# A four-layer graph network on one core: the prologue in a new order, and six more steps of the second pair's front inside it

## The chip, the cores and the metric

The kernel runs on one core of a Trainium2 chip (trn2). The core has TensorE (PE) for matrix products, VectorE (DVE), ScalarE (ACT) and GpSimd (POOL) for elementwise work and reductions, and SyncE (SP), which issues transfers; ScalarE issues transfers too. Each engine runs its own instructions in the order in which the program gives them. The metric is the device time of one execution in microseconds; lower is better.

## The reference

Thirty-two graphs `x` of 512 nodes with 64 features share one weighted adjacency matrix `adj` (512 x 512). Four layers follow each other, each as `x = x + layer(relu(layernorm(x)))`:

```python
# layer 0, three steps; node 0 is first set to an intervention value
effects = einsum('nm,bmd->bnd', adj, v)
v = relu(concat([v, effects]) @ W1.T + b1) @ W2.T + b2
# layer 1, twice
z = relu((adj @ z) @ weights[i])
# layer 2, eight heads, then the same once more with W_out
h = x @ W;  s = (h @ h.T) * graph;  s = where(s == 0, -1e16, s)
out = softmax(s) @ h + b          # leaky_relu(0.01) after it
# layer 3; adj has its diagonal set to 1
h = x @ weight;  e = leaky_relu(e_src + e_dst, 0.2) * adj
out = softmax(e) @ h + bias
```

Layers 2 and 3 hold most of the work: for every graph nine 512 x 512 score matrices with a softmax over the graph in layer 2, and one in layer 3.

## The kernel before

Two graphs are worked on together as a pair; there are 16 pairs. Nodes lie on the partitions in four blocks of 128, and the two graphs' features lie side by side, 128 wide. Everything is in float32, except for the mask (`NEGM`) and the small identity (`I2b`), which are bfloat16.

The program has three parts. A **prologue** issues the loads and prepares shared operands. The **ticks**, ten for each pair, hold the attention work: in every tick each unit of heads has its scores (L427, and L430 for the mask), maxima (L448), exponentials (L459), normalisations (L471), turns (L477) and weighted sums (L487). The order inside a tick is written out by hand in a table, `PLACES`: a step's name gives the tick that it belongs to and its place there. A **tail** finishes the last pair.

Layers 0 and 1 of a pair are a generator, `front(p, state)`, whose 24 yields cut it into steps counted from 0. Steps 0 and 1 are the first normalisation, 2 its end, 3 a transpose. Each of the three steps of layer 0 is three front steps: `by_nodes` (L329) into PSUM; `v` copied by ScalarE (L353) or added to `ubc` by VectorE (L355); then L363 and `aggregated` (L317) into one bank and ReLU to `hT` (L366). These are front steps 4 to 12. Step 13 adds the residual (`x1`, L370) and issues the load of the pair after next. Steps 14 to 16 normalise (VectorE: L264, L266, L273, L275, L281; POOL: L268, L270, L277), 17 to 20 are layer 1 (L317, `eT` at L380, L329 with `NP`; `x2` at L388), 21 to 23 normalise again. At the end `features_of` transposes z (L401, ZZ at L403) and `values_of` issues the 16 transfers of `quarters` (L299). The keys of the attention (L804, Y at L814) come before the scores.

In the ticks the front of the next pair is spread over the table as names `F0` to `F24`. The first pair's front runs in the prologue, and the second pair's first six steps are called there too, one after each of the first pair's steps 6 to 11 (`HEAD = 6`); its further steps, from `F6`, lie in the ticks of the first pair.

Between the first pair's steps the prologue calls the functions that prepare operands, by the dictionary `among`: `weights_turned` (L175 to L180: W1 and W2 transposed, copied to W1T and W2T by ScalarE), `biases` (L191 to L193), `weights_joined` (L198 to L204: products of W2 with W1 and with the biases), `graph_turned` (L186, L187: 16 transposes of `A` and four copies to `AT` by ScalarE), `masks` (L209 to L212), `factors` (L230: one quarter each of the graph copy `A2`), `grams` (L237 to L243), `vectors` (L247 to L255).

Transfers are issued from two queues. SP loads x of the first pair, `A` (L124), x of the second, then NP (L143), Wh (L145), A2 (L147), the small weights of layer 3 (L149 to L151), W_out (L152) and A3 (L154). ScalarE loads W1 (L132), W2 (L133), the bias rows (L136, L137), the intervention value (L139) and b2 spread over the partitions (`b2bc`, L140). In the program each transfer takes one of eight completion counters in turn, and waits until the transfer before it on the same counter has landed.

Of the kernel before, what the change touches and what calls it, by code (L numbers as in the profile page):

```python
# [9 lines left out]
BF16 = mybir.dt.bfloat16  # L10
AF = mybir.ActivationFunctionType
ALU = mybir.AluOpType
AX = mybir.AxisListType

P = 128
# [6 lines left out]
def gnn_stack_kernel(  # L22
# [36 lines left out]
    nc = tc.nc  # L59
    B, N, D = x.shape  # L60
# [8 lines left out]
    R = tuple(slice(j * D, (j + 1) * D) for j in range(2))  # L69

    def blk(t):
        return slice(t * P, (t + 1) * P)

    def hblk(s):
        return slice(s * D, (s + 1) * D)

    const = ctx.enter_context(tc.tile_pool(name="const", bufs=1))
# [8 lines left out]
    def mm_ps():  # L86

        return ps_m.tile([P, N], F32, tag="mm", name="mm")
# [16 lines left out]
    ident = const.tile([P, P], F32, name="ident")  # L105
    mhalf = const.tile([P, NT * 2], F32, name="mhalf")
    ivt = const.tile([1, 2, D], F32, name="ivt")

    early1 = hp.tile([P, 4, P], F32, tag="h3T", bufs=1, name="early1")
    W1n, W2n, ones = early1[:, 0:2], early1[:, 2], early1[:, 3]  # L110
# [9 lines left out]
    rows, b2rep = early2[0:NB, 0], early2[:, 1]  # L120
# [6 lines left out]
    make_identity(nc, ident)  # L127
    for z0, value in ((mhalf, -0.5), (ones, 1.0), (NP, 0.0), (w3a, 0.0), (a1bd, 0.0), (a2bd, 0.0)):
        nc.gpsimd.memset(z0, value)
    for j, r in enumerate(R):  # L130
        for k in range(2):
            nc.scalar.dma_start(out=W1n[r, k, r], in_=W1[:, k * D : (k + 1) * D])  # L132
        nc.scalar.dma_start(out=W2n[r, r], in_=W2)  # L133
    for k, b in enumerate((b1, b2, b_out, bias3)):
        for r in R:
            nc.scalar.dma_start(out=rows[H + k : H + k + 1, r], in_=b.rearrange("(o d) -> o d", o=1))  # L136
    nc.scalar.dma_start(out=rows[0:H, :], in_=bh)  # L137
    for j in range(2):
        nc.scalar.dma_start(out=ivt[:, j, :], in_=iv)  # L139
        nc.scalar.dma_start(out=b2bc[:, 0, j, :], in_=b2.partition_broadcast(P))  # L140
    xts[1] = load_x(1)
    for r in R:
# [15 lines left out]
    W1T = const.tile([P, 2, 2, P], F32, name="W1T")  # L158
    W2T = const.tile([P, P], F32, name="W2T")
    cols = const.tile([P, NB], F32, name="cols")  # L160
    b1c, b2c, boc, b3c = (cols[:, H + k : H + k + 1] for k in range(4))
    ubc = const.tile([P, 1, P], F32, name="ubc")
    b1s = const.tile([P, 1], F32, name="b1s")
    b1k = (b1c, b1s)
    AT = const.tile([P, NT, N], F32, name="AT")
    II = const.tile([P, 2, D], F32, name="II")
    II2 = II.rearrange("p k d -> p (k d)")
    I2b = const.tile([P, D], BF16, name="I2b")
    NEGM = const.tile([P, NT, N], BF16, name="NEGM")
    a2rep = const.tile([P, P], F32, name="a2rep")  # L170
    G = const.tile([P, H, D], F32, name="G")
# [10 lines left out]
    def graph_turned():  # L182
        for s in range(NT):
            pt = mm_ps()
            for t in range(NT):
                nc.tensor.transpose(pt[:, blk(t)], A[:, t, blk(s)], ident)  # L186
            nc.scalar.copy(AT[:, s, :], pt)  # L187

    def biases():
        pt = mm_ps()  # L190
# [4 lines left out]
    def weights_joined():  # L195
        pt = mm_ps()
        for k in range(2):
            nc.tensor.matmul(pt[:, blk(k)], lhsT=W2n, rhs=W1T[:, k, 0, :], start=True, stop=True)  # L198
        nc.tensor.matmul(pt[:, 2 * P : 3 * P], lhsT=b2rep, rhs=W1T[:, 1, 0, :], start=True, stop=True)
        nc.tensor.matmul(pt[:, 3 * P : 3 * P + 1], lhsT=W1T[:, 0, 0, :], rhs=b2c, start=True, stop=True)  # L200
        for k in range(2):
            nc.vector.tensor_copy(W1T[:, k, 1, :], pt[:, blk(k)])
        nc.vector.tensor_copy(ubc[:, 0, :], pt[:, 2 * P : 3 * P])
        nc.vector.tensor_tensor(b1s, pt[:, 3 * P : 3 * P + 1], b1c, ALU.add)  # L204

    def masks():

        for k in range(2):
            nc.vector.tensor_tensor(II[:, k, :], ident[:, 0:D], ident[:, D:P], ALU.add)  # L209
        nc.vector.tensor_copy(I2b, II[:, 0, :])  # L210

        nc.vector.tensor_scalar(NEGM, A, 0.0, NEG_INF, ALU.is_equal, ALU.mult)  # L212

# [14 lines left out]
    def factors(k):  # L228
        a2 = A2[:, 2 * k : 2 * k + 2, :]
        nc.vector.scalar_tensor_tensor(a2, a2, 0.0, a2, ALU.is_equal, ALU.add)  # L230

    def grams():

        WT = hp.tile([P, H, D], F32, tag="us", bufs=1, name="WT")
        pt = mm_ps()
        for h in range(H):
            nc.tensor.transpose(pt[:, hblk(h)], Wh2[0:D, h, :], ident[0:D, 0:D])  # L237
        nc.vector.tensor_copy(WT.rearrange("p h d -> p (h d)"), pt)
        pt = mm_ps()
        for h in range(H):  # L240
            for r in R:
                nc.tensor.matmul(pt[r, hblk(h)], lhsT=WT[:, h, :], rhs=WT[:, h, :], start=True, stop=True)
        nc.vector.tensor_copy(G.rearrange("p h d -> p (h d)"), pt)  # L243

    def vectors():
        for j in range(2):
# [549 lines left out]
    def keys(ua, ub):  # L796
# [22 lines left out]

    state = {p: {} for p in range(NPAIR)}  # L820
    first, second = front(0, state), front(1, state)
    HEAD = 6
    among = {
        0: [weights_turned],
        1: [biases, weights_joined, graph_turned],
        7: [masks],
        8: [lambda: factors(0)],
        9: [lambda: factors(1)],
        10: [lambda: factors(2)],
        11: [lambda: factors(3)],  # L830
        14: [grams],
        15: [vectors],
    }
    for n, _ in enumerate(first):
        for fn in among.get(n, ()):
            fn()
        if 6 <= n < 6 + HEAD:
            next(second)


# [80 lines left out]
    def at(t, name, fn):  # L921
        dt, place = PLACES.get(name, (1, 0))
        if t + dt < LEAD and name[0] in "FZ":

            dt, place = LEAD - t, PLACES["s1a"][1] + 0.01 * (len(jobs[LEAD]) + 1)
        token = f"{owner[0]}:{name}"
        if token in TAIL and (t + dt >= END or owner[0] in list("epqrsEU")):
            dt, place = END + 1 - t, TAIL.index(token)
        jobs.setdefault(t + dt, []).append((place, fn))
# [34 lines left out]
    for p in range(NPAIR):  # L964
# [31 lines left out]
        if p + 1 < NPAIR:  # L996
            steps = second if p == 0 else front(p + 1, state)
            for n in range(HEAD if p == 0 else 0, 25):
                at(base, f"F{n}", lambda steps=steps: next(steps, None))
# [50 lines left out]
```

## Time and profile before

| what | value |
|---|---|
| median of 3 runs | 2333.57 us (2332.89 to 2333.98) |
| profiled execution | 2338.17 us, span 2336.3 us |
| mean granted TensorE clock | 0.976 |
| TensorE busy | 2186.7 us, 94% of the span |
| VectorE busy | 1857.4 us, 80% |
| ScalarE busy | 1493.1 us, 64% |
| POOL busy | 1299.6 us, 56% |
| first scores (L427) of the first pair start | 82.88 us |
| first weighted sum (L487) starts | 107.82 us |
| TensorE busy from 200 to 300 us | 99.10 of 100 us |

The page describes one execution in microseconds. A line such as `L317` is a line of the kernel; `mm<-AT,v` names the tile written and those read. In the slices the span is cut into 40 equal parts, each digit the busy share in tenths. The list of windows gives busy microseconds (and instructions) of TensorE, its weight loads, VectorE, ScalarE and POOL in a stretch, then the granted clock, the share of time in which the transfer engines were busy, and GB/s. The chain of waits goes back from the last instruction to what released it, step by step.

### The profile page before, as it was taken

The page shows a single profiled execution, that of the slowest core. Times are in us where ns is not written, and L with a number is a line of the kernel's source. Part 1 is how long each engine was busy: PE and PEld are TensorE (multiplying, and loading weights), DVE is VectorE, ACT ScalarE, POOL GpSimd, SP SyncE. Part 2 cuts the span into 40 slices and gives each one's busy share as a digit, 9 for nine tenths or more (in the row PEclk, how much of TensorE's full clock was granted, in tenths as well). Part 3 has the DMA queues.
Part 4 walks back from the last instruction along what each step waited for, and adds up shares of the span by engine and source line. Part 5 has one row for each costly group of instructions (what it writes and reads, how often), then busy time and mean ns, then how long its engine had stood idle before and what let it go on. Part 6 is the DMA issues. An engine that isn't in the chain of part 4 may idle for free.

```text
span 2336.3 us, 78517 instructions
## 1 busy us (share of the span) xinstructions
PE 2186.7 (94%) x32683; PEld 1172.3 (50%) x32683; DVE 1857.4 (80%) x4100; ACT 1493.1 (64%) x3752; POOL 1299.6 (56%) x2175
## 2 busy tenths in 40 slices
PE   6889999999999999999999999999999999999863
PEld 3435555555555555555555555555555555555342
DVE  3558788879888888988888898888888898887653
ACT  1346557667676766767676676767666676766544
POOL 2345465656666565565656466565656556655342
PEclk9899999999999999999999999999999999999886
DMA  5001111202121120212112021211202111211112
GB/s 122 11 15 21 25 20 23 42 14 39 21 41 26 24 42 13 41 21 39 25 27 40 13 42 21 37 25 29 39 15 42 20 31 25 31 32 19 22 25 46
DMA packets 279047, 70.20 MB, mean 30 GB/s; under 512 B 275100, under 2 KB 276132, under 8 KB 278692
## 3 DMA queue, kind: packets, MB, share of 16 engines
q1 hardware_dynamic: 277888, 65.02, 16.8%
q8 instruction: 256, 4.19, 0.8%
q14 instruction: 99, 0.81, 0.1%
q10 hardware_dynamic: 804, 0.17, 0.0%
HBM read 10.49 MB, written 4.19 MB: 6 GB/s over the span
## 4 chain that ended last, share of the span: by engine, by line
PE 76%; ACT 9%; DVE 6%; POOL 2%; SPq 2%; issue 1%; DMA 1%; ACTq 0%; DVEq 0%; POOLq 0%
PE s L427 20%; PE mm L487 17%; PE mm L317 9%; ACT sm L459 6%; PE mm L550 5%; PE mm L756 5%; PE mm L521 5%; PE s L430 5%; DVE sm L477 4%; PE mm L329 3%; PE mm L804 3%; SPq L299 2%; PE mm L363 1%; DVE sm L448 1%; PE mm L593 1%
## 5 line engine op out<-in xcount | busy, mean ns | idle before, releaser
L459 ACT ACTIVATE sm<-sm,nmx 128x512 f32<-128x512 f32 x1280 | 911.0, 720 | 238.5 <-POOL nmx L455 238.2
L471 POOL TENSOR_SCALAR sm<-sm,rs 128x512 f32<-128x512 f32 x1280 | 869.8, 699 | 149.1 <-DVE rs L469 109.0
L448 DVE CUSTOM_DVE_ANT_0 sm<-s,A 128x512 f32<-128x512 f32 x1152 | 734.0, 679 | 146.3 <-PE s L430 119.8
L477 DVE STREAM_TRANSPOSE sm<-sm 128x1024 f32<-128x1024 f32 x640 | 769.4, 1224 | 39.5 <-POOL sm L471 38.4
L427 PE MATMUL s<-ZZ,Y 64*64 64x512 f32 x4096 | 572.1, 605 | 24.9 <-ACT Y L814 14.0
L487 PE MATMUL mm<-sm,vq 32*64 32x256 f32 (+1 forms) x17152 | 502.7, 380 | 26.0 <-DVE sm L477 18.3
L455 POOL TENSOR_SCALAR nmx<-mx 128x2 f32<-128x2 f32 x640 | 148.3, 235 | 600.6 <-DVE mx L448 544.7
L487 PEld LDWEIGHTS mm<-sm,vq 32*64 32x64 f32 x17152 | 401.8, 135 | 141.7 <-issue 55.9
L427 PEld LDWEIGHTS s<-ZZ,Y 64*64 64x64 f32 x4096 | 146.9, 132 | 250.2 <-issue 112.9
L430 PE MATMUL s<-NEGM,I2b 64*64 64x512 bf16 x2304 | 257.9, 378 | 0.0
L459 ACT ACTIVATION_READ_ACCUMULATOR sm<-sm,nmx 128x1 f32 x1280 | 251.2, 196 | 0.0
L542 ACT COPY us<-mm 128x256 f32<-128x256 f32 x256 | 76.2, 382 | 156.6 <-PE mm L487 156.4
L317 PE MATMUL mm<-AT,v 128*128 128x512 f32 x384 | 173.6, 595 | 0.0
L532 ACT ACTIVATE y<-mm,cols 128x512 f32<-128x512 f32 x256 | 159.2, 684 | 11.1 <-PE mm L521 11.0
L268 POOL TENSOR_TENSOR xc<-x,nmu 128x512 f32<-128x512 f32 x48 | 54.8, 1141 | 192.1 <-DVE nmu L266 192.1
L430 PEld LDWEIGHTS <-I2b 64*64 64x64 bf16 x2304 | 81.0, 107 | 159.8 <-issue 159.2
L521 PE MATMUL mm<-us,Wh 64*64 64x512 f32 x1024 | 133.9, 592 | 23.1 <-ACT us L542 23.1
L277 POOL TENSOR_TENSOR r<-ve,mhalf 128x8 f32<-128x8 f32 x64 | 110.8, 1731 | 44.9 <-DVE ve L275 41.1
L756 PE MATMUL mm<-sm,vq 32*64 32x256 f32 x3712 | 118.0, 380 | 10.2 <-DVE sm L477 8.8
L550 PE MATMUL mm<-y,Wo_sb 128*64 128x512 f32 x512 | 126.9, 605 | 0.0
L317 PE MATMUL mm<-AT,z 128*128 128x512 f32 x256 | 120.1, 613 | 2.1 <-DVE z L281 1.4
L317 PEld LDWEIGHTS mm<-AT,v 128*128 128x128 f32 x384 | 73.2, 191 | 93.3 <-issue 91.7
(134 smaller groups left out, 2002.0 us busy)
## 6 DMA issues: line engine op xcount, KB each, us to landing
vq<-z SPq DMA_DIRECT2D x512, 32.0 KB, 1.9
vq<-hn SPq DMA_DIRECT2D x512, 32.0 KB, 1.9
vq<-h3n SPq DMA_DIRECT2D x512, 32.0 KB, 1.9
A<-in_adj_dram SPq DMA_DIRECT2D x5, 1024.0 KB
xt<-in_x_dram SPq DMA_DIRECT2D x32, 128.0 KB, 2.3
out_dram<-xo SPq DMA_DIRECT2D x32, 128.0 KB, 2.9
src<-src SPq DMA_DIRECT2D x64, 1.0 KB, 1.9
Wh<-in_L_gnn_Wh_dram SPq DMA_DIRECT2D x2, 256.0 KB
```

What stands on the lines that cost most here:

```text
L317: nc.tensor.matmul(pe, lhsT=v[:, m].rearrange("p j d -> p (j d)"), rhs=AT[:, m, :], start=(first and m == 0), stop=(m == NT - 1),)
L427: nc.tensor.matmul(pss[half][R[ab], :], lhsT=lhsT, rhs=rhs, start=True, stop=False)
L430: nc.tensor.matmul(pss[half][R[ab], :], lhsT=I2b[R[half], :], rhs=NEGM[R[half], k, :], start=False, stop=True,)
L448: nc.vector.tensor_tensor_reduce(self.sm[:, s, :], src, graph, 1.0, -FMAX, ALU.mult, ALU.max, self.mx[:, s : s + 1])
L459: nc.scalar.activation(self.sm[:, s, :], self.sm[:, s, :], AF.Exp, bias=self.nmx[:, s : s + 1], accum_out=self.ssum[:, s : s + 1],)
L471: nc.gpsimd.tensor_scalar(self.sm[:, s, :], self.sm[:, s, :], self.rs[:, s : s + 1], 1.0, ALU.mult, ALU.mult)
L477: nc.vector.transpose(out=two, in_=two)
L487: nc.tensor.matmul(self.u[i][R[c], 0 : weights.shape[1] * 32], lhsT=values[32 * i : 32 * i + 32, jb, :], rhs=weights[32 * i : 32 * i + 32, ...
L521: nc.tensor.matmul(py[c][r, :], lhsT=Wh2[R[c], 2 * (self.q - 1 + c) + ab, r], rhs=self.us[R[c], 2 * ab : 2 * ab + 2].rearrange("p i (s e) ...
L532: nc.scalar.activation(y, py[c], AF.Prelu, bias=cols[:, h : h + 1], alpha=0.01)
L550: nc.tensor.matmul(pa[R[ab], :], lhsT=Wo_sb[:, h, :], rhs=self.y[h], start=(k == 0), stop=(k == 1),)
L756: nc.tensor.matmul(self.u[i][r, 0 : N // 2], lhsT=values[i // 2][q, jb, :], rhs=sm[q, :, 32 * jb : 32 * jb + 32], start=(jb == 0), stop=(j ...
```

## The change

Arithmetic and results stay; the order of the prologue changes, and who does some of its copies.

- W1 is loaded with one transfer for each half of the partitions instead of two. The intervention value is loaded earlier.
- `I2b` is copied by ScalarE straight from the identity, between its transfers, and no longer cast on VectorE in `masks`.
- `graph_turned` runs before `biases` and `weights_joined`; two of its four copies go to VectorE. `weights_joined` is cut in two: the part with the biases becomes `biases_joined` and runs four steps later.
- `grams` copies on ScalarE instead of VectorE.
- `masks` moves from step 7 to 9, the four `factors` from 8 to 11 to 16 to 19, `vectors` from 15 to 17.
- Twelve steps of the second pair's front run in the prologue instead of six: the new ones (`F6` to `F11`, two `by_nodes`, two `v`, two aggregations with `hT`) stand after the first pair's steps 14, 15, 16, 21, 22 and 23. They leave the ticks of the first pair.

```diff
-    for j, r in enumerate(R):
-        for k in range(2):
-            nc.scalar.dma_start(out=W1n[r, k, r], in_=W1[:, k * D : (k + 1) * D])
+    for r in R:
+        nc.scalar.dma_start(out=W1n[r, :, r], in_=W1.rearrange("o (k d) -> o k d", k=2))
         nc.scalar.dma_start(out=W2n[r, r], in_=W2)
+    for j in range(2):
+        nc.scalar.dma_start(out=ivt[:, j, :], in_=iv)
+
+    I2b = const.tile([P, D], BF16, name="I2b")
+    for r in R:
+        nc.scalar.copy(I2b[r], ident[r, r])
     for k, b in enumerate((b1, b2, b_out, bias3)):
         for r in R:
             nc.scalar.dma_start(out=rows[H + k : H + k + 1, r], in_=b.rearrange("(o d) -> o d", o=1))
     nc.scalar.dma_start(out=rows[0:H, :], in_=bh)
     for j in range(2):
-        nc.scalar.dma_start(out=ivt[:, j, :], in_=iv)
         nc.scalar.dma_start(out=b2bc[:, 0, j, :], in_=b2.partition_broadcast(P))
...
-            nc.scalar.copy(AT[:, s, :], pt)
+            (nc.scalar.copy, nc.vector.tensor_copy)[s % 2](AT[:, s, :], pt)
...
-        nc.tensor.matmul(pt[:, 2 * P : 3 * P], lhsT=b2rep, rhs=W1T[:, 1, 0, :], start=True, stop=True)
-        nc.tensor.matmul(pt[:, 3 * P : 3 * P + 1], lhsT=W1T[:, 0, 0, :], rhs=b2c, start=True, stop=True)
-        for k in range(2):
             nc.vector.tensor_copy(W1T[:, k, 1, :], pt[:, blk(k)])
-        nc.vector.tensor_copy(ubc[:, 0, :], pt[:, 2 * P : 3 * P])
-        nc.vector.tensor_tensor(b1s, pt[:, 3 * P : 3 * P + 1], b1c, ALU.add)
+
+    def biases_joined():
+        pt = mm_ps()
+        nc.tensor.matmul(pt[:, 0:P], lhsT=b2rep, rhs=W1T[:, 1, 0, :], start=True, stop=True)
+        nc.tensor.matmul(pt[:, P : P + 1], lhsT=W1T[:, 0, 0, :], rhs=b2c, start=True, stop=True)
+        nc.vector.tensor_copy(ubc[:, 0, :], pt[:, 0:P])
+        nc.vector.tensor_tensor(b1s, pt[:, P : P + 1], b1c, ALU.add)
...
-        nc.vector.tensor_copy(I2b, II[:, 0, :])
...
-        nc.vector.tensor_copy(WT.rearrange("p h d -> p (h d)"), pt)
+        nc.scalar.copy(WT.rearrange("p h d -> p (h d)"), pt)
...
-        nc.vector.tensor_copy(G.rearrange("p h d -> p (h d)"), pt)
+        nc.scalar.copy(G.rearrange("p h d -> p (h d)"), pt)
...
-    HEAD = 6
+
+    BESIDE = (6, 7, 8, 9, 10, 11, 14, 15, 16, 21, 22, 23)
+    HEAD = len(BESIDE)
     among = {
         0: [weights_turned],
-        1: [biases, weights_joined, graph_turned],
-        7: [masks],
-        8: [lambda: factors(0)],
-        9: [lambda: factors(1)],
-        10: [lambda: factors(2)],
-        11: [lambda: factors(3)],
+        1: [graph_turned],
+        2: [weights_joined],
+        3: [biases],
+        5: [biases_joined],
+        9: [masks],
         14: [grams],
-        15: [vectors],
+        16: [lambda: factors(0)],
+        17: [lambda: factors(1), vectors],
+        18: [lambda: factors(2)],
+        19: [lambda: factors(3)],
     }
     for n, _ in enumerate(first):
         for fn in among.get(n, ()):
             fn()
-        if 6 <= n < 6 + HEAD:
+        if n in BESIDE:
             next(second)
```

More of the change, by code (lines that the diff above doesn't have):

```diff
@@ L167, in gnn_stack_kernel @@
     II2 = II.rearrange("p k d -> p (k d)")
-    I2b = const.tile([P, D], BF16, name="I2b")
     NEGM = const.tile([P, NT, N], BF16, name="NEGM")
```

## The prediction

> **What bounds the kernel now.** I read the page's busy table and slices first. TensorE is 94% busy, and its row of the slices shows where it isn't: the first slices and the last.
>
> ```profile
> PE 2186.7 (94%) x32683; PEld 1172.3 (50%) x32683; DVE 1857.4 (80%) x4100; ACT 1493.1 (64%) x3752; POOL 1299.6 (56%) x2175
> PE   6889999999999999999999999999999999999863
> PEclk9899999999999999999999999999999999999886
> ```
>
> So TensorE work is dear after the ramp and nearly free in the prologue (0 to 82.9 us). The chain that ended last, in order of time, shows what the prologue waits for. Columns: start, length, what.
>
> ```profile
> 3.62 5.95 DMA early<-in_L_gnn_W_dram
> ...
> 26.27 5.25 DMA Wo_sb<-in_L_gnn_W_out_dram
> 31.52 1.22 DVE A L230
> ...
> 42.59 0.70 DVE x L370
> ...
> 50.14 6.71 PE mm L317 x8
> ...
> 64.98 0.70 DVE x L388
> ...
> 76.78 2.00 PE mm L363 x2
> 78.78 4.17 PE mm L317 x8
> ...
> 100.21 3.45 PE mm L317 x8
> ```
>
> The reader sees a serial chain: weights until 9.6; a graph copy (A2) that lands at 31.5 and holds VectorE; two normalisations (from 42.59 and 64.98) in which TensorE waits; then a piece of the second pair's front (76.78 to 82.95) ahead of the first scores. L317 takes 6.71 us at 50.14 and 3.45 later, for the same eight records. The windows say why: busy time by engine, then the granted clock.
>
> ```profile
> 42.60:50.10 7.50, 2.68 (x43) 2.13 (x43) 4.96 (x12) 0.00 (x0) 3.73 (x3) 0.73 0.17 37
> 50.10:65.00 14.90, 12.71 (x32) 5.89 (x32) 0.02 (x1) 1.77 (x3) 0.00 (x0) 0.79 0.00 0
> 65.00:73.00 8.00, 0.00 (x0) 0.00 (x0) 3.08 (x6) 0.00 (x0) 4.33 (x4) 0.59 0.00 1
> 73.00:82.90 9.90, 9.22 (x34) 3.99 (x34) 0.00 (x0) 1.66 (x3) 0.00 (x0) 0.64 0.30 49
> 96.00:108.00 12.00, 11.10 (x70) 4.77 (x74) 11.44 (x23) 7.38 (x21) 6.75 (x14) 1.00 0.01 1
> ```
>
> TensorE idles 5 us and 8 us, and comes back at a clock of 0.6 to 0.8. From 96 to 108 VectorE, too, is full (11.44 of 12).
>
> The list of waits on ScalarE for the first 45 us has one more:
>
> ```profile
> ACT L179 <- DMA ivt<-_intervention_value_dram: 12.5, 1, 12.5
> ```
>
> ScalarE issues 19 transfers itself. Its first compute stands behind all of them, with the 1.28 us table load (12.53 to 13.81); only then is W1T copied.
>
> **What the Trainium skill says.** "TensorE: Matmul & The Clock Gate", Part 1, says that an idle TensorE falls to half its clock after about 3.4 us and needs about as long of activity to come back: the trace agrees (8.06 us idle, then L363 at 2.07 for 1.02). The same part calls ScalarE's and VectorE's queues strict FIFO, so a waiting instruction holds all behind it; the trace agrees (L281 and L309 behind L230 at 31.5). "DMA: Bandwidth & Descriptors", Anatomy of one DMA, says that a transfer's semaphore wait happens on the issuing sequencer: the trace agrees (SP's xt waits 5.9 us for a weight). Its fixed cost of about 2.0 us fits xt (2.3 to landing), not the weights (5.9) or NP (4.2).
>
> **The change part by part.**
>
> *Transfers.* In both programs each transfer takes one of eight completion counters in turn and waits for the one before on that counter. Two transfers fewer (2 x 0.62 us of issue) shift every later assignment. W1's bytes stay, so weights land about 9.5 as now. Then ScalarE, in order: ivt; table load and two I2b copies (not in the trace; 0.19 to 0.43 each by the ScalarE copies there, I take 0.25; hidden, since all end near 6 and the weights land at 9.5; uncovered they cost 0.5, not less than nothing); b1 waits for the last W2 (9.5); the second b2 waits for xt1 (issued near 8.4, +2.3: 10.7); b_out waits for both NP transfers (issued 8.8 to 10.3, +4.2: 13 to 14.5); bias3 and bh by 15; b2bc waits for the second Wh half. Wh is queued behind NP on SP; its first half took from 12.46 to 20.4 now, with A2 and b2bc in flight. In the new order A2 itself waits for Wh, so I take 16.5 and bound it 14.5 to 20. The W1T copies then start near 17.0 (bounds 15 to 20.5), against 13.82. That is an added wait; behind it on ScalarE stand W1T, W2T, AT and zT, and TensorE and all the first pair wait for zT.
>
> *Graph turned first.* The 16 transposes (3.3 us) run from 9.5, when A has landed, instead of 15.87. VectorE takes two of the four AT copies (2 x 0.58). zT then starts 0.43 + 0.28 + 1.16 = 1.9 after W1T: 18.9, against 19.69, a gain of 0.8. biases_joined now lies between by_nodes and L363: 0.63 + 0.43 us of records, 0.85 on TensorE's path. Sum: 0; the first hT stays at 25.9.
>
> *factors moved.* At 31.52 L230 held z of the second pair, so L309 and L329 began 1.1 later than hT allowed (33.07 to 34.21). The four factors (4 x 1.2) now follow the first z of the norm, where A2 is long there: gain 1.1. If b2bc lands late (18.07 now, perhaps 22), POOL's L337, xc and sq and then VectorE's v and ve run 4 us later and end near 27.5, still just ahead of L355 at 27.85. x1 comes at 41.5 (42.59). The cast of I2b (about 0.15) leaves VectorE at a place with slack: nothing.
>
> *First normalisation*, counted from x1. z is ready at +7.45, now as before. TensorE: Wh transposes to +0.6, WT copy on ScalarE to +1.25, Gram matmuls to +2.45, then the second pair's L363 and L317 (0.9 + 3.45) to +6.75, hT on ScalarE to +7.5, by_nodes to +8.7. So L317 of the first pair starts at +8.7 instead of +7.55, but warm: 3.7 instead of 6.7. Then w3's transpose and L254, which waits for w3T behind VectorE's a2rep, hold L329 0.8 longer than eT would. x2 comes at +21.0, now +22.39. Gain 1.4.
>
> *Second normalisation.* x2 to the end of z's copy stays at 7.98. L363, L317, hT and by_nodes (6.3) fit in; VectorE's v stands behind z and costs nothing there, since scores need Y later. L401 (1.11 to 0.6) and L804 (1.98 to 1.1) run warm: 1.4 less. L363 and L317 are gone from between keys and scores: 6.2 less (76.71 to 82.88). Instead the scores wait for Y, which those hid: 1.0 more. Gain 6.6.
>
> So the first scores come 1.1 + 1.4 + 6.6 = 9.1 earlier, at 73.8.
>
> *Ramp.* Steps F6 to F11 leave the ticks: L363 and L317 at 99.1 (4.6), two by_nodes (2 x 1.1), two v (2 x 0.65), hT. That is 6.8 us of TensorE, but VectorE sets the pace from 84 to 108, so the gain is its own: 0.9 where by_nodes delayed the third pair of scores (88.00), 0.6 for v at 106.62. I take 1.3 (0.3 to 5: nothing but v if the rest refills, nearly all of TensorE's share if VectorE catches up). From the first weigh (107.82) both orders are the same, TensorE is 99% busy, and the lead is kept.
>
> Sum: 9.1 + 1.3 = 10.4. The profiled execution has 2338.17 us around its span of 2336.3, 0.2% over the median of 2333.57; so it would become 2327.8, and the median **2323.2**.
>
> **Rivals.**
>
> *1, likeliest (0.72).* As worked out: a gain of 7 to 13, by W1T at 15 to 19.5 and the ramp's bounds.
>
> *2, late transfers (0.14).* Wh or NP land as late as now, W1T starts at 20 to 23, b2bc comes so late that POOL holds VectorE's v. For it: a Wh half took 7.9 us. Against: A2's 2 MB are no longer beside it. 3 to 6 us lost of 10.4: about 2328.5.
>
> *3, more comes through (0.08).* Transfers land in 2.3 us each, so W1T starts at 14 (3 us more), and TensorE's freed time counts in the ramp (2 more): 2317 to 2319.
>
> *4, slower (0.04).* ScalarE stands at b2bc until Wh's second half lands, and that comes only after the A2 halves, which landed at 26.3 and 31.4. Every us of W1T after 17.0 passes to the end; the gain is gone from 27.4, and with W1T at 32.5 the time is 10.4 - 15.5 = 5 us worse: 2338.7. Against: Wh is issued ahead of A2, and the first A2 half waits for the first Wh half.
>
> *5, it does not do what it says (0.02).* TensorE's fillers don't keep the clock up, or the lead is absorbed at a later wait on VectorE (126 to 131): within 0.2%. For: VectorE is 80% busy. Against: its order there is unchanged, so it leads too.
>
> **Numbers.** A measurement can tell about 0.2% (4.7 us) from no change, so faster means under 2328.9. Case 1, case 3 and most of case 2 are faster: 0.90. The rest of 2, and 5: 0.06. Case 4: 0.04. The range runs from case 3's 2317.5 to case 2's 2328.5.
>
> **What would show it.** In the new profile: AT's transposes from about 9.5; W1T copies at 15 to 19.5 with a wait on transfers just before; no VectorE wait on A2; L317 of the first z at 3.7 us and a clock near 1.0 from 42 to 80; x2 near 62.5; first scores near 74; the first weigh near 97.4. W1T after 22, or cold L317s after the norms, would make the forecast wrong; so would a first weigh later than 104.

## The result and the profile after

| | before | after |
|---|---|---|
| median of 20 runs | 2333.66 us (2329.20 to 2336.53) | 2329.24 us (2325.23 to 2334.82) |
| profiled execution, span | 2338.17, 2336.3 us | 2334.82, 2333.0 us |

The ratio is 0.9984, 95% interval 0.9978 to 0.9991: 4.4 us by the medians, where 10.4 were forecast, and the median lies above the range of 2317.5 to 2328.5. The profiled execution of after is the longest of its twenty, so its times are read against other executions further down. Lines of after stand four further on than those of before from L230 on: L317 is now L321, L329 L333, L363 L367, L366 L370, L370 L374, L388 L392, L427 L431, L448 L452, L487 L491, L521 L525.

The page of after: busy table, TensorE's slices, granted clock.

```profile
PE 2189.5 (94%) x32683; PEld 1170.6 (50%) x32683; DVE 1857.3 (80%) x4099; ACT 1493.9 (64%) x3754; POOL 1298.6 (56%) x2175
PE   7889999999999999999999999999999999999873
PEclk9899999999999999999999999999999999999886
```

The averages barely move: TensorE is 2.8 us busier with the same work, and the clock's second slice is still an 8. The chain of waits of after, its first 140 us (start, length, what):

```profile
9.96 3.74 DMA Wh<-in_L_gnn_Wh_dram
...
14.13 10.14 DMA b2bc<-in_L_gnn_b_dram
24.41 1.26 POOL xt L341
...
27.82 0.70 DVE v L277
...
28.71 0.60 DVE v L359
29.36 3.71 PE mm L321 x8
...
43.54 1.88 PE mm L246 x32
45.42 1.92 PE mm L367 x2
...
64.47 0.70 DVE x L392
...
75.95 1.99 PE s L431 x8
78.37 1.71 PE s L431 x8
...
102.61 10.04 PE mm L491 x248
...
129.05 8.92 PE mm L491 x250
```

The graph copy A2 and the lone L363 and L317 ahead of the scores are gone; the scores start 6.9 us earlier than in the first profile of before (82.88). In their place the chain shows b2bc, which lands at 24.3 and holds POOL, then VectorE's v. The products at half clock ("cold" from here on, "warm" at full clock) are still there, at other places: L246 and L367 at 43.5 to 47.3, the first scores at 1.99 for eight (1.02 warm), and the first two weighted sums at 10.04 and 8.92 (7.80 for 256 and 7.15 for 250 in before).

Windows of after (busy us of TensorE, its loads, VectorE, ScalarE, POOL; granted clock; transfers):

```profile
42.60:50.10 7.50, 6.83 (x46) 3.99 (x45) 3.30 (x7) 1.17 (x2) 3.73 (x3) 0.77 0.15 35
50.10:65.00 14.90, 12.15 (x47) 6.48 (x46) 6.00 (x10) 2.46 (x4) 0.00 (x0) 1.00 0.01 2
65.00:73.00 8.00, 5.39 (x21) 2.72 (x19) 3.17 (x7) 0.69 (x1) 4.34 (x4) 1.00 0.00 0
73.00:82.90 9.90, 8.56 (x62) 3.06 (x64) 2.80 (x9) 3.06 (x7) 0.44 (x2) 0.66 0.31 50
96.00:108.00 12.00, 9.56 (x136) 4.63 (x140) 10.42 (x22) 2.93 (x8) 7.67 (x15) 0.74 0.00 1
```

The steps beside the normalisations do fill TensorE (6.83 of 7.5 us where it had 2.68; 5.39 of 8 where it had nothing). But the clock is 0.77 beside the first normalisation, 0.66 from 73 to 83, and 0.74 from 96 to 108, a stretch that ran at 1.00 before. In the second normalisation the added steps end at 70.7 us (L333 at 69.51 for 1.16), before the wait does. Finer windows of the same ramp in after:

```profile
92.50:96.00 3.50, 1.86 (x16) 0.50 (x12) 2.97 (x7) 3.49 (x10) 1.23 (x3) 1.00 0.00 0
96.00:99.00 3.00, 2.29 (x16) 0.50 (x12) 2.97 (x7) 0.00 (x0) 3.00 (x6) 1.00 0.00 0
99.00:102.50 3.50, 1.88 (x16) 0.51 (x16) 3.50 (x6) 1.95 (x5) 1.70 (x5) 0.89 0.00 0
102.50:106.00 3.50, 3.39 (x64) 2.28 (x72) 1.96 (x8) 0.98 (x4) 1.60 (x4) 0.50 0.02 5
```

With steps F6 to F11 gone from the ticks TensorE is only half to three quarters busy while it waits for VectorE. No wait there is longer than 1.6 us, yet the clock falls, at 101.73 us, and the weighted sum that follows runs at half speed. Windows laid on the two falls, the stretch ahead of each and then the cold one:

```profile
71.01:74.42 3.41, 1.25 (x16) 0.89 (x20) 1.29 (x2) 0.58 (x1) 0.64 (x2) 1.00 0.12 19
74.42:81.25 6.83, 6.16 (x40) 1.95 (x32) 2.04 (x7) 1.07 (x2) 0.23 (x1) 0.50 0.33 53
98.32:101.73 3.41, 2.09 (x18) 0.51 (x16) 3.41 (x6) 1.18 (x3) 2.38 (x6) 1.00 0.00 0
101.73:108.56 6.83, 5.95 (x112) 3.95 (x120) 5.28 (x12) 2.13 (x7) 3.12 (x6) 0.50 0.01 2
```

### The profile page after: what moved, and what is told of

It reads as the page before. It is cut to its first block, busy times and chain, and to the rows that moved or that the text cites. A ratio compares the mean times of both kernels' runs of the same rounds, so it can differ in the third digit from the quotient of the medians.

```text
span 2333.0 us, 78520 instructions
## 1 busy us (share of the span) xinstructions
PE 2189.5 (94%) x32683; PEld 1170.6 (50%) x32683; DVE 1857.3 (80%) x4099; ACT 1493.9 (64%) x3754; POOL 1298.6 (56%) x2175
## 4 chain that ended last, share of the span: by engine, by line
PE 76%; ACT 9%; DVE 7%; POOL 3%; SPq 2%; issue 2%; DMA 1%; ACTq 0%; DVEq 0%; POOLq 0%
PE s L431 20%; PE mm L491 16%; PE mm L321 9%; ACT sm L463 6%; PE mm L554 5%; PE mm L525 5%; PE mm L760 5%; PE s L434 5%; DVE sm L481 4%; PE mm L333 3%; PE mm L808 3%; SPq L303 2%; DVE sm L452 2%; PE mm L367 1%; PE mm L597 1%
## 5 line engine op out<-in xcount | busy, mean ns | idle before, releaser
L452 DVE CUSTOM_DVE_ANT_0 sm<-s,A 128x512 f32<-128x512 f32 x1152 | 734.5, 680 | 145.0 <-PE s L434 118.9
L431 PE MATMUL s<-ZZ,Y 64*64 64x512 f32 x4096 | 574.9, 606 | 28.7 <-ACT Y L818 14.7
L491 PE MATMUL mm<-sm,vq 32*64 32x256 f32 (+1 forms) x17152 | 504.3, 381 | 28.9 <-DVE sm L481 20.2
L491 PEld LDWEIGHTS mm<-sm,vq 32*64 32x64 f32 x17152 | 400.1, 135 | 147.4 <-issue 59.1
L431 PEld LDWEIGHTS s<-ZZ,Y 64*64 64x64 f32 x4096 | 147.5, 132 | 257.2 <-issue 110.9
L321 PE MATMUL mm<-AT,v 128*128 128x512 f32 x384 | 173.1, 593 | 0.1
L536 ACT ACTIVATE y<-mm,cols 128x512 f32<-128x512 f32 x256 | 159.3, 684 | 11.0 <-PE mm L525 10.9
L525 PE MATMUL mm<-us,Wh 64*64 64x512 f32 x1024 | 134.0, 592 | 23.2 <-ACT us L546 23.2
L760 PE MATMUL mm<-sm,vq 32*64 32x256 f32 x3712 | 118.1, 380 | 10.2 <-DVE sm L481 8.8
L321 PEld LDWEIGHTS mm<-AT,v 128*128 128x128 f32 x384 | 73.3, 191 | 93.5 <-issue 92.6
L285 DVE SCALAR_TENSOR_TENSOR z<-xc,r 128x512 f32<-128x512 f32 x64 | 45.3, 708 | 92.6 <-POOL r L281 89.4
```

What stands on the lines that cost most here:

```text
L321: nc.tensor.matmul(pe, lhsT=v[:, m].rearrange("p j d -> p (j d)"), rhs=AT[:, m, :], start=(first and m == 0), stop=(m == NT - 1),)
L431: nc.tensor.matmul(pss[half][R[ab], :], lhsT=lhsT, rhs=rhs, start=True, stop=False)
L452: nc.vector.tensor_tensor_reduce(self.sm[:, s, :], src, graph, 1.0, -FMAX, ALU.mult, ALU.max, self.mx[:, s : s + 1])
L491: nc.tensor.matmul(self.u[i][R[c], 0 : weights.shape[1] * 32], lhsT=values[32 * i : 32 * i + 32, jb, :], rhs=weights[32 * i : 32 * i + 32, ...
L525: nc.tensor.matmul(py[c][r, :], lhsT=Wh2[R[c], 2 * (self.q - 1 + c) + ab, r], rhs=self.us[R[c], 2 * ab : 2 * ab + 2].rearrange("p i (s e) ...
L536: nc.scalar.activation(y, py[c], AF.Prelu, bias=cols[:, h : h + 1], alpha=0.01)
```

## A ledger of the prologue

A mark in the trace closes each stage, so the lengths of a row add up to the last mark. "Fifth maximum" is the fifth L448 (L452 in after), where VectorE begins to run without gaps; "products" the third L521 (L525), the first mark behind both weighted sums. Rows that follow from experiments are named after them.

| kernel | x1 | x1 to x2 | x2 to scores | scores to fifth maximum | to the products | mark at |
|---|---|---|---|---|---|---|
| before, first profile | 42.59 | 22.39 | 17.90 | 5.12 | 51.97 | 139.97 |
| before, mean of four profiles | 42.08 | 22.00 | 17.39 | 5.12 | 51.97 | 138.56 |
| forecast | 41.5 | 21.0 | 11.3 | (with the next) | 55.8 | 129.6 |
| after, first profile | 42.27 | 22.20 | 11.48 | 6.77 | 55.94 | 138.66 |
| after, e10 | 42.95 | 20.63 | 12.04 | 5.85 | 52.08 | 133.55 |
| after, e14 | 42.89 | 20.62 | 12.49 | 6.83 | 55.99 | 138.82 |
| after, e16 | 43.60 | 22.17 | 11.63 | 6.63 | 55.82 | 139.85 |
| e3, nine steps | 43.88 | 20.62 | 12.49 | 5.79 | 51.98 | 134.76 |
| e4, products repeated | 42.25 | 20.62 | 11.15 | 4.23 | 51.38 | 129.63 |
| e12, ramp alone | 43.38 | 22.11 | 11.66 | 6.59 | 51.37 | 135.11 |
| e8, all warm, b2bc early | 39.17 | 20.62 | 11.13 | 4.23 | 51.37 | 126.52 |

The first profile of after loses in the two stages behind the scores (1.65 and 3.97 us) nearly all that it won before them. From the 37th turn on VectorE (217 to 233 us) to the 561st (2000 to 2015 us) every kernel here takes about the same (1781.5 to 1783.5 us). What follows the 561st turn is called the tail below.

## The experiments

The theory: moving TensorE's work out of the ramp starves it there, its clock falls, and the freed time is paid back. Rivals: the new order alone is what brings the gain, or costs it (b2bc); the forecast was too large because the profile of before was no typical execution. "Own before" is the median of before's runs in the same comparison, with 95% intervals for the ratio.

**The change in two halves.** e1 is after with only the six old steps beside the first pair; e2 is before with the twelve.

```diff
# e1, in after
-    BESIDE = (6, 7, 8, 9, 10, 11, 14, 15, 16, 21, 22, 23)
+    BESIDE = (6, 7, 8, 9, 10, 11)
# e2, in before
-    HEAD = 6
+    BESIDE = (6, 7, 8, 9, 10, 11, 14, 15, 16, 21, 22, 23)
+    HEAD = len(BESIDE)
...
-        if 6 <= n < 6 + HEAD:
+        if n in BESIDE:
```

> The new prologue order with only the six old steps of the second pair's front beside the first pair (steps F6 to F11 stay in the ticks). Clock theory (the gain was lost because TensorE, emptied of F6 to F11 in the ramp, falls to half its clock there): the front by itself brings x1 some 0.3 to 1 us earlier and the factors no longer hold it; the ramp stays dense, first weighted sum at 7.7 to 8 us. About 2332.5 us, 0 to 2 us under before. Front theory (the new order of transfers loses what the fillers gain): 3 to 5 us over before, about 2337.

> The kernel before with nothing changed but the twelve steps of the second pair's front beside the first pair's steps 6 to 11, 14 to 16 and 21 to 23. Clock theory: nearly all of the measured gain is here, 3 to 5 us under before (2329 to 2331), with a cold first weighted sum (9 us or more) in the profile. Front theory: the fillers alone give the forecast 9 us, about 2324.5.

Measured: e1 2334.61 us, ratio 1.0001 (0.9993 to 1.0010); e2 2334.16 us, 0.9998 (0.9989 to 1.0007); own before 2334.38. By the medians neither half does anything alone. For e1 that is at the edge of what was expected (0 to 2 us under before); its x1, at 42.58, is not earlier. For e2 it is a miss: its profile is the shortest of its 13 executions (2328.87 us, the others up to 2340.89), so that nothing shows where the others lose; even there the first weighted sum lasts 8.50 us.

**Nine steps.** e3 leaves F9 to F11 in the ticks.

```diff
-    BESIDE = (6, 7, 8, 9, 10, 11, 14, 15, 16, 21, 22, 23)
+    BESIDE = (6, 7, 8, 9, 10, 11, 14, 15, 16)
```

> The changed kernel, but with nine steps of the second pair's front in the prologue instead of twelve: F6, F7 and F8 beside the first normalisation; F9 to F11 back in the ticks, so that they stand among the scores again and nothing fills the second normalisation. Clock theory: the ramp, whose pace VectorE sets, hides F9 to F11 and TensorE keeps its clock at the first weighted sum (7.7 to 8 us), but idles through the second normalisation and starts the scores cold: within 2 us of the changed kernel, 2327 to 2331. Rival, that all moved TensorE work comes through: F9 to F11 cost their 4.6 + 1.1 + 0.6 us again, 3 us or more over the changed kernel, 2332 to 2335.

Measured: 2329.11 us (ten runs, 2327.23 to 2330.40), ratio 0.9976 (0.9967 to 0.9986), own before 2334.38: 5.3 us, and a spread of 3 us instead of 10 (e11 below, with the same nine steps, spreads over 7.7). Windows of e3 in the ramp:

```profile
92.50:96.00 3.50, 3.50 (x20) 1.37 (x14) 3.03 (x7) 3.50 (x11) 1.18 (x3) 1.00 0.00 0
99.00:102.50 3.50, 3.29 (x32) 1.74 (x32) 3.50 (x6) 2.02 (x6) 1.78 (x5) 1.00 0.00 0
102.50:106.00 3.50, 3.50 (x116) 2.63 (x120) 2.61 (x8) 1.07 (x4) 0.94 (x3) 1.00 0.02 5
```

and TensorE's timeline there (start, length, what):

```profile
102.60 7.80 PE L491 MATMUL mm<-sm,vq 32*64 32x256 f32 x256
126.81 7.15 PE L491 MATMUL mm<-sm,vq 32*64 32x256 f32 x250 [1.26 <-DVE x L374]
```

VectorE is as busy as in after (3.50 of 3.5 us from 99), but TensorE is too, the clock stays at 1.00, and the sums take 7.80 and 7.15. The second normalisation gets cold instead (TensorE 0.47 of 8 us from 65 to 73, at 0.60), which costs about 1 us of x2 to scores against the first profile of after. By the medians, F9 to F11 cost nothing where they stood; the intervals of e3 and after overlap.

**Products repeated to keep TensorE warm.** e4 issues products twice, in after: those of the last `by_nodes` of the second pair's first twelve steps, and the products of the third unit's score blocks. Results are those of the second time.

```diff
-        for t in range(NT):
+        for t in list(range(NT)) * times:
...
-            pv = by_nodes(hT, W1T[:, 1, k, :])
+            pv = by_nodes(hT, W1T[:, 1, k, :], 2 if p == 1 and step == 2 else 1)
...
+            again = getattr(self, "again", 1)
+            for half in list(range(2)) * (again - 1):
+                for ab in range(2):
+                    lhsT, rhs = operands(half, ab)
+                    nc.tensor.matmul(pss[half][R[ab], :], lhsT=lhsT, rhs=rhs, start=True, stop=True)
...
+            self.again = 2 if (p, j, q) == (0, 0, 2) else 1
```

> The changed kernel with more work for TensorE: the second pair's last by_nodes before the scores is done twice, and the first products of the third unit's four score blocks are done twice (same operands, same result), 1.1 + 4 x 0.86 = 4.5 us of added matmuls, put where TensorE waits. Clock theory: TensorE keeps its full clock at the first scores and at the first weighted sum (7.7 to 8 us instead of 10), and the time is 2 to 5 us under the changed kernel, 2324 to 2327, with less spread between runs. Rival, that the clock is an accident without weight or that the ramp has no room: 0 to 4.5 us over the changed kernel, 2329 to 2334.

Measured: 2327.91 us (six runs), ratio 0.9970 (0.9959 to 0.9982), own before 2334.38: 6.5 us, about 2 more than after has over its own before, the lower edge of what the theory expected. Windows of e4 in the ramp, then its timeline (L496 is the weighted sum):

```profile
92.50:96.00 3.50, 3.30 (x32) 1.11 (x33) 3.50 (x7) 0.00 (x0) 3.50 (x7) 1.00 0.00 0
102.50:106.00 3.50, 3.50 (x104) 2.35 (x92) 2.04 (x4) 2.23 (x7) 0.57 (x2) 1.00 0.02 5
```

```profile
98.14 7.13 PE L496 MATMUL mm<-sm,vq 32*64 32x256 f32 x248 [0.67 <-DVE sm L486]
121.68 7.15 PE L496 MATMUL mm<-sm,vq 32*64 32x256 f32 x250 [1.26 <-DVE x L374]
```

More work on TensorE, and every stage from x1 on is as short as forecast or shorter: the mark falls at 129.63, where the forecast put 129.6. That is the strongest sign for the theory; but the intervals of e4 and after still overlap.

**The ramp alone.** e12 is e4 without the repeated `by_nodes`.

> The changed kernel in which only the first product of each of the four score blocks of the third unit is issued twice (L427; the results are those of the second); the second normalisation is as in the changed kernel. Theory (the ramp alone is where the moved steps are paid back): first weigh 7.8 us instead of 10.04, second 7.15 instead of 8.79, 1 to 3 us under the changed kernel: 2326 to 2328.3. Rival (the loss is in the second normalisation, 74 to 81 us, at half clock, and the ramp only inherits it): within 0.7 us of the changed kernel.

Measured: 2330.98 us, ratio 0.9993 (0.9985 to 1.0001), own before 2332.49. The sums are warm (7.14 and 7.15), as the theory had it, but the time is not below after's; by the ratios it is some 2 us above it, which is nearer to the rival's reading than to the theory's. The ledger shows 22.11, and 6.59 behind the scores: L246 and the scores at half clock, as in the first profile of after. It should still have shown some 3 us by the ledger; its tail took part of that (below).

**b2bc early.** e5 issues b2bc right behind the intervention value, in after.

```diff
     for j in range(2):
         nc.scalar.dma_start(out=ivt[:, j, :], in_=iv)
+        nc.scalar.dma_start(out=b2bc[:, 0, j, :], in_=b2.partition_broadcast(P))
...
-    for j in range(2):
-        nc.scalar.dma_start(out=b2bc[:, 0, j, :], in_=b2.partition_broadcast(P))
```

> The changed kernel with b2 spread over the partitions (b2bc) loaded right after the intervention value instead of last. Late-transfer theory: POOL's addition of b2bc starts near 12 to 18 us instead of 24.4, the second pair's normalisation no longer holds VectorE's v, and x1 comes 0.5 to 1.5 us earlier; the time is 1 to 2 us under the changed kernel (2327 to 2328.5). Clock theory: what the front gains or loses by that is within 1 us, and the spread by TensorE's clock is larger; within 1.5 us of the changed kernel. If the weights land later because b2bc reads beside them, W1T starts later and the gain is eaten: 0 to 2 us over it.

Measured: 2328.90 us (21 runs, 2322.96 to 2333.10), ratio 0.9979 (0.9971 to 0.9986), own before 2333.63: 4.7 us. POOL's wait for b2bc goes (its addition is at 10.9 instead of 24.4), and x1 comes at 39.94, 2.3 earlier. Not all of that is POOL's wait: ScalarE's W1T copies no longer stand behind the late issue of b2bc and start at 13.61 instead of 14.83, and the first hT is at 24.35, already 2.2 earlier. But the sums take 10.06 and 8.80 again, and little of the 2.3 is left at the end.

**Before with a warm TensorE, and after with all of it warm.** e6 puts eleven products that nobody reads into before's normalisations. e7 is e4 with such products at two more places, ahead of W1T and before the scores of the sixth unit (146 to 153 us); e8 is e7 with b2bc early.

```diff
# e6, in before
+    def spare(times, lhsT, rhs):
+        pt = ps_s.tile([P, N], F32, tag="s", name="spare")
+        for k in range(times):
+            nc.tensor.matmul(pt, lhsT=lhsT, rhs=rhs(k % NT), start=True, stop=True)
...
-        14: [grams],
-        15: [vectors],
+        14: [grams, lambda: spare(2, W2T, lambda k: AT[:, k, :])],
+        15: [vectors, lambda: spare(2, W2T, lambda k: AT[:, k, :])],
+        21: [lambda: spare(7, W2T, lambda k: AT[:, k, :])],
# e7, in e4, with a spare() that takes another PSUM bank where its last argument is True
-        1: [graph_turned],
+        1: [graph_turned, lambda: spare(2, ident, lambda k: A[:, k, :])],
...
+            jobs.setdefault(base + 7, []).append((50, lambda: spare(7, W2T, lambda k: AT[:, k, :], True)))
```

> The kernel before, with spare matmuls (nothing reads them) while TensorE waits in the first pair's two normalisations: 4 in the first, 7 in the second, 0.86 us each. Nothing else changes. Clock theory: part of what the fillers of the change bring is only the clock; the first L317 after the norm takes 3.7 us instead of 6.7 and the keys and the first scores run at full clock: first scores 4 to 6 us earlier in the profile, and 2 to 4 us under before in the median, since in some executions before is warm there by itself. Rival, that the work moved is what counts: within 1 us of before.

> The changed kernel with the repeated products of e4_warm, and spare matmuls in two more places where TensorE waits: 2 after the graph's transposes (13 to 15 us), 7 before the scores of the sixth unit (near 146 to 153 us). Clock theory: no cold stretch from 13 us to the tail; the first hT 1 to 2.5 us earlier than in e4_warm, 2 to 3 us more at the cold scores near 153: 2322 to 2325. Rival: the added matmuls are in the way, or those stretches have slack: 2327 to 2330 as e4_warm.

> e7_all_warm with b2bc loaded right after the intervention value, as in e5_b2bc_early. Late-transfer theory: with TensorE warm in the front the late b2bc is what orders it, so this brings 1 to 2 us over e7_all_warm. Clock theory alone: the same as e7_all_warm within 1 us.

| | median us (runs) | ratio (95%) | own before |
|---|---|---|---|
| e6 | 2336.26 (21) | 1.0014 (1.0008 to 1.0021) | 2333.63 |
| e7 | 2326.38 (6) | 0.9970 (0.9959 to 0.9982) | 2333.63 |
| e8 | 2323.25 (5) | 0.9958 (0.9945 to 0.9970) | 2333.63 |

e6 is a miss: its cold stretches shrink to 3.4 us each and the mark comes at 137.01, but its time is 2.6 us longer. Warm normalisations are worth little in before; e6's tail is the longest of all (325.9 us). e7 brings hT forward (24.31 instead of 26.53), then waits for b2bc like after (the next hT at 32.67); its gain of 7.3 us is only 0.8 above e4's, and the time stays above the 2322 to 2325 expected. e8 takes that wait away too and is 10.4 us under its own before, the best version here, below both kernels. Where TensorE is warm the early b2bc brings 3.1 us by the medians (2326.38 to 2323.25), more than was expected, though with six and five runs the intervals overlap. The chain of waits of e8 (L396 is x2, L440 the first scores):

```profile
51.62 0.50 issue
52.12 0.35 PE mm L262 x2
...
59.79 0.70 DVE x L396
...
70.92 1.09 PE s L440 x8
```

The first scores follow x2 by 11.1 us and run warm, at 70.92.

**Nine steps and b2bc early.** e11 joins e3 and e5, with no product repeated.

> The changed kernel with nine of the twelve steps (F9 to F11 stay in the ticks) and the two b2bc transfers issued right behind those of the intervention value; no product is repeated. Theory (F9 to F11 keep TensorE's clock in the ramp, so a start that is earlier by 2.3 us passes through to the end, as it did with repeated products: 3.1): 2325.5 to 2327.5 us, first weigh at 7.8 us, ratio 0.996 to 0.997. Rival (an earlier start is lost again, as with twelve steps, where 2.3 us brought under 1): 2328 to 2329.5.

Measured: 2325.96 us, ratio 0.9975 (0.9966 to 0.9984), own before 2332.49: 6.5 us. The time and the 7.79 us of the first sum are the theory's, but own before was 1.9 us lower here than beside e3, so that b2bc brings about 1.2 us over e3's 5.3, and the two intervals are nearly the same; the ratio of 0.996 to 0.997 was not reached. Between theory and rival this leaves it open. It has the lowest median of the versions without idle work.

**Both programs profiled again.** Unchanged: e9, e13 and e15 are before, e10, e14 and e16 after.

> The kernel before, unchanged, profiled a second time. Theory (which stretches of the prologue run at half clock differs between executions of one program, and the first profile of before fell on a dear one, 4.5 us over its median): this execution takes 2330 to 2336 us, its first products after the first normalisation (L317, 6.71 us for eight at 50.14 in the first profile) take 3.5 to 5.5 us at least in one of the two normalisations, and the first weigh stands 1 to 4 us earlier than 107.82. Rival (the cold stretches belong to the program): cold from 46 to 56 and from 66 to 80 again, L317 at 6.4 to 6.9 us, the first weigh within 1 us of 107.8; then a gain of 10 from the new order should have been seen, and something later in the program took it.

> The changed kernel, unchanged, profiled a second time. Theory (chance decides which of the half-empty stretches loses the clock): 2325 to 2333 us, and not the same six cold stretches from 16 to 163 us; the second weigh (129.05, 8.79 us in the first profile) starts at 123 to 128, if the second normalisation or the first weigh stayed warm. Rival (the same stretches every time): cold from 74 to 81, 102 to 108 and 129 to 132 again, the second weigh at 128.5 to 129.5.

> The kernel before, unchanged, third profile, read by the marks of the prologue alone. Theory (the first profile was a late one, and the forecast took its marks as typical): first weigh at 104 to 106.5 us as in the second profile (105.11). Rival (the second was an early one): 107.3 to 108.5. In both, the stretch from the first normalisation (near 42 to 53) and that from the second (near 66 to 77) are at half clock.

> The changed kernel, unchanged, third profile. Theory (the clock is lost somewhere between 70 and 132 us in every execution, at a place that varies): first or second weigh longer than 7.8 and 7.15 us, or the first scores at 2.0 for eight; third product of L525 at 133 to 139 us, where 129.6 is what a warm execution has. Rival (a warm execution is common and the tail takes the gain): 129 to 131 us.

> As for the third profile of before: first weigh at 104 to 106.5 us by the theory, 107.3 to 108.5 by the rival; the tail (from the 561st turn on VectorE to the end of the span) 318 to 322 us by either.

> As for the third profile of after: third product of L525 at 133 to 139 us by the theory, 129 to 131 by the rival; the tail 318 to 320 us by the theory, 322 or more by the rival.

Measured: before 2332.32, 2334.47 and 2332.92 us, first weighted sum at 105.11, 107.03 and 105.69 us; after 2328.80, 2333.95 and 2334.50 us, the mark at 133.55, 138.82 and 139.85. The chain of waits of e9 shows L317 after the first normalisation:

```profile
49.63 5.24 PE mm L317 x8
...
63.00 0.70 DVE x L388
...
80.23 1.02 PE s L427 x8
```

It took 6.71 us in the first profile. Both normalisations are at half clock in every profile of before, so the rival of e9 was right that these stretches belong to the program; the mark varies by 2.7 us between them, and the first profile was the latest of four, 1.4 us over their mean. (e13 falls between the two windows that were set for it; the mark of e16 lies 0.85 us beyond the 139 that was set for it.) For after, the timelines of e14 and e10:

```profile
102.72 10.07 PE L491 MATMUL mm<-sm,vq 32*64 32x256 f32 x248 [1.53 <-DVE sm L481]
129.20 8.80 PE L491 MATMUL mm<-sm,vq 32*64 32x256 f32 x250 [1.26 <-DVE x L374]
```

```profile
100.28 8.92 PE L491 MATMUL mm<-sm,vq 32*64 32x256 f32 x256
125.60 7.15 PE L491 MATMUL mm<-sm,vq 32*64 32x256 f32 x250 [1.25 <-DVE x L374]
```

Three profiles in four run parts of both sums at half clock (times 2333.95 to 2334.82, the mark no earlier than the mean of before); one pays 1.1 us in the first alone, and has 2328.80. Of the twenty runs in the comparison 12 were under 2330. The tails are 321.7, 318.7, 319.4 and 318.3 us in before and 319.1, 318.9, 318.7 and 318.4 in after: the tail doesn't take the gain of after.

## Why the prediction was wrong, step by step

**Right.** TensorE turns A from 9.57 us and VectorE no longer waits for A2. W1T starts even earlier than the bounds of 15 to 20.5, at 14.83 (14.82 to 16.37 in the four profiles), and zT at 17.50. The first normalisation gives 1.4 us over the mean of before in the profiles where L246 stays warm (20.62 against 22.00), as forecast, though the parts that the forecast lists add up to only 1.1; x2 to scores gives 4.9 to 5.9 of the forecast 6.6, and 6.2 with TensorE warm. The lead is kept in the middle part.

**The step that failed first: "a clock near 1.0 from 42 to 80", and with it "the gain is its own" in the ramp.** I took filled slots as warm slots, and freed TensorE time under a pace set by VectorE as free. I had used what "TensorE: Matmul & The Clock Gate", Part 1, says of a TensorE idle for about 3.4 us, and left out that the same part sets the clock by how busy TensorE has been recently. After shows no such gap: TensorE was busy for 1.25 of 3.41 us ahead of the scores and for 2.09 of 3.41 ahead of the first sum, with waits up to 1.8, and the clock behind each stretch was 0.50. I had read the 1.00 of before in the ramp as given, when the six moved steps helped to keep it. Instead of gaining 1.3, after loses 1.5 to 1.7 behind the scores and 3.9 to 4.0 in the sums in three profiles of four, and 0.73 and 0.11 in the fourth. The first loss comes from the second normalisation (behind the scores e12, without the repeated `by_nodes` there, takes 6.59 us, e4, with it, 4.23), the second from the ramp: e3 and e11 (steps left there), e4 and e12 (products repeated there) all bring the sums back to 7.1 to 7.8.

**Second: the start.** zT does come earlier (17.50 to 19.30 in the four profiles, 19.46 to 20.66 in before), but L333 and L367 run cold behind it. TensorE's timeline of after:

```profile
18.14 2.08 PE L333 MATMUL mm<-W1T,zT 128*128 128x128 f32 x8 [0.47 <-ACT zT L315]
20.72 2.06 PE L367 MATMUL mm<-zT,W1T 128*128 128x512 f32 x2
27.27 1.16 PE L333 MATMUL mm<-W1T,hT 128*128 128x128 f32 x8 [0.78 <-ACT hT L370]
28.27 1.02 PE L367 MATMUL mm<-hT,W1T 128*128 128x512 f32 x2
```

Turning the graph first leaves TensorE empty from 13 us until W1T; with two unread products there, e7 has hT at 24.31. So hT is at 26.53, and at 27.30 to 28.01 in the other three profiles, not at 25.9 (25.67 to 26.88 in before). And the gain of 1.1 for `factors` could be had in the first profile of before alone. From the first hT to x1 that one takes 16.68 us, the other three 15.59 to 15.66, and after 15.58 to 15.74. The wait shows at L309, here in the first profile and then in e9, where it is gone:

```profile
33.74 0.63 PE L309 MATMUL mm<-ident,z 128*128 128x128 f32 x4 [1.45 <-DVE z L336]
32.17 0.63 PE L309 MATMUL mm<-ident,z 128*128 128x128 f32 x4
```

POOL's wait list of after holds b2bc,

```profile
POOL xt L341 <- DMA b2bc<-in_L_gnn_b_dram: 14.4, 1, 14.4
```

which lands at 24.3. I had allowed 22, with v and ve done by 27.5; VectorE's v at 27.82 and L359 at 28.71 hold the second aggregation, there and in e16; in e10 and e14 L359 waits for the cold L333 instead. x1 is at 42.27 to 43.60, no earlier than the mean of before (42.08). With b2bc early it is at 39.94 (e5) and 39.17 (e8), which counts POOL's wait and ScalarE's earlier W1T together. One citation was misplaced: the fixed cost of about 2.0 us in "DMA: Bandwidth & Descriptors", Anatomy of one DMA, is that of transfers issued by GpSimd, and here SP and ScalarE issue them; no time of the forecast rests on it.

**Third: the sum's baseline.** I set the gain against one execution and shifted the result by 0.2%, which makes the time typical but not the stages. That execution had the latest prologue of four; 1.4 of the 10.4 us lay in it, the wait at `factors` among them.

Together: against the mean of before the forecast mark (129.6) means 9.0 us. The favourable execution of after, e10, has 5.0 and the median gain is 4.4; the other three have between 0.1 us lost and 1.3 lost. e4 has 8.9 there. So about 1.4 us of the forecast was the baseline. Of the rest, the mark of e10 shows where it went: it comes 3.9 us behind the forecast, 1.4 of them at x1 (42.95 for 41.5), 0.7 from x2 to the scores (12.04 for 11.3) and 2.1 behind these (57.93 for 55.8), less 0.4 won between x1 and x2. The marks show that the sums follow the clock; that the time does isn't shown as firmly, since the intervals of e3, e4 and after overlap and e12, with warm sums, gained 1.5 us, less than after.

**The rivals.** 5 named the right mechanism ("TensorE's fillers don't keep the clock up"), at 0.02, and with a loss of everything; what came is a mixture of it and 1. Of 2, the late b2bc came true, though W1T was early. By the bound of 0.2% that I had set, the gain stands at its edge: 2329.24 us, against 2328.9.

**Open.** By the medians e4 and e7 gain 6.5 and 7.3, not 8.9 or more, and e6 loses. Why e2, with all the fillers and the old start, gains nothing by its median isn't known. The 10.4 us of e8 equal the forecast by chance: e8 has products and an early b2bc that the forecast didn't count. The tails of the five kernels with repeated or unread products last 320.6 to 325.9 us, those of the other thirteen profiles 317.5 to 321.7, with the same instructions. One profile of each doesn't tell chance from cause; the tail's own half-speed stretches add up to 72 to 94 us in every kernel, and no run took them apart.

## What to carry to other kernels

Work that is taken from an engine which waits for another isn't always free to take: look at how busy the stage leaves TensorE, and leave fillers where little else keeps it busy (here 54% of a stretch lost the clock, 94% kept it). Before a gain below half a per cent is summed from single stages, read those stages in several executions. Two halves of a change that each bring nothing can bring something together, as here by the medians, and that nine steps of twelve do no worse than all was found only by trying it.

## What the runs showed of the hardware

- TensorE lost its clock without a gap of 3.4 us: behind 2.09 of 3.41 us busy (after, 98.32 to 101.73) and behind 1.53 of 3.42 us busy (e10, 92.58 to 96.00), with waits up to 1.6 us, it was 0.50. At 3.29 to 3.50 of 3.5 (e3, e4) it kept 1.00. In the first 200 us of all 18 profiles the clock fell 59 times, each time behind a stretch of 3.41 us in which TensorE was busy for 66% or less; some stretches of 51 to 66% kept it.
- Half-speed stretches in the first 200 us lasted 3.4, 6.8, 10.2 or 13.7 us in all traces that have any, and in one program they fell differently from execution to execution: e10 has its mark 5.3 us ahead of e14, and a time 5.2 us shorter.
- The second of two broadcasts of 256 bytes to 128 partitions, issued at 14.1 us beside the loads of A2, took 10.1 us to land; with both issued right behind the intervention value (e8) b2bc was in use at 10.2.
